# Silu of the recurrence's inputs and its gate as one ScalarE function, in pairs, and padded images that share their zero columns

## The chip, the cores and the metric

The kernel runs on one core of a Trainium2 chip. The metric is device microseconds (us) from launch to end; the median of three runs of the kernel before is 14450.43 us (14435.74 to 14463.01). The engines of the core work side by side, each through its own queue in order: TensorE (PE, matmuls, with its weight loads PEld), VectorE (DVE), ScalarE (ACT, table functions), GpSimd (POOL), and SyncE (SP), which here only issues transfers (DMA).

## The reference

32 images of 128 channels and 56 x 56 pixels, in float32, pass through four layers, each with a residual:

```python
# L0: group norm, then a 1x1 convolution whose weights are mixed per image by a small attention,
#     then three depthwise 3x3 convolutions with dilations 1, 3, 5
y = einsum('boi,bihw->bohw', agg_w, x) + agg_b
for dil in (1, 3, 5):
    out = out + silu(conv_general_dilated(y, ds_weight, padding=dil, rhs_dilation=dil) + ds_bias)
# L1: group norm, then a cubic B-spline of every element
# L2: group norm, linear attention over 8 heads, then a depthwise 3x3 convolution (dilation 1)
# L3: layer norm, then a selective state space recurrence along the 3136 pixels
xin, z = split(einsum('blc,ec->ble', xn, in_proj_w), 2)
xc = silu(conv_b + sum(xp[:, k:k + L] * conv_w[:, k] for k in range(4)))
dt, B, C = split(x_proj_w @ xc);  delta = softplus(dt_proj_w @ dt + dt_proj_b)
h = exp(delta * A) * h + delta * B * xc;  y = C . h + D * xc        # 256 channels x 16 states
out = out_proj_w @ (y * silu(z))
```

The change is about the two silu of L3, `silu(conv ...)` and `silu(z)`, and about the images with zero borders that L0 and L2 store for their depthwise convolutions.

## The kernel before

An image is held as 128 partitions (channels) by 3136 pixels and cut into seven chunks of 448 pixels (8 rows). Of each chunk the recurrence takes 16 steps; a step handles two groups of 128 rows (32 channels by 4 states each). Over 32 images this makes 224 chunks and 3584 steps. In one step:

- ScalarE computes the decays `da` with two Exp of 448 columns (`decay`); three buffers `da` take turns, so the decays of a step wait for the scan of three steps before;
- TensorE spreads the B row over the partitions into the PSUM tile `pb` (`b_rows`), and for every other step the C row, which ScalarE copies to `cb`;
- VectorE multiplies `rep` (a copy of delta*x that a transfer spread) with `pb` into `db`, which lies in one PSUM buffer, and runs `tensor_tensor_scan` over 904 columns into `h` (`state`);
- GpSimd multiplies `h` with `cb` into `hc` (`products`), and TensorE sums `hc` into `y` (`add`).

Around these steps lies all other work, of this chunk and of other images. `ssm_inputs` ("next") prepares the following chunk: 16 matmuls per half with the input projection (`winT`), silu into `xc`, the projection to `dbl`, softplus into `delta` and `du`, two transfers to DRAM, from which `rep` is fetched, and the layer norm of the chunk after that. `gate` ("gate") makes `sz = silu(z)`. "rest" is the spline and attention of the next image, and "conv" the L0 layer of the image after that.

A planner (`Plan`) sets the order. Every call is recorded as a `Work` with a price and a due time; `LEAD` shifts the due times by kind of work; `attempt` then takes, for each engine, the work that can begin first, where a work that needs another ScalarE table than the one loaded counts 0.6 us later. The order that comes out is written into each engine's queue and is fixed. The program's main loop (line 1505) covers six images a turn, five times, and the last two images follow.

`silu` computes with the tanh of half the argument: the weights `winT` and `wzT` are halved once at the start, ScalarE takes Tanh of the PSUM tile into `t`, and VectorE computes `(t + 1) * ps`. Because VectorE reads the PSUM tile too, the bias of the convolution has to be in it: a matmul of `cbT` (in the type float32r, with a high and a low part of the bias in rows 0 and 32) by a column of ones, broadcast over 448 columns, adds it. Tanh lies in the same table as Exp; Ln, used in softplus and in the layer norm, lies in another.

`padded` are two DRAM images with a border of five zeros on every side: rows of 66 floats. `store_rows` writes eight rows (seven in L2) through a buffer `yc`, and `load_stack` reads three shifted copies of eight rows for one depthwise convolution, 528 floats per channel each.

Of the kernel before, what the change touches and what calls it, by code (L numbers as in the profile page):

```python
# [13 lines left out]
F32 = mybir.dt.float32  # L14
# [5 lines left out]
P = 128  # L20
# [5 lines left out]
HALO = 5  # L26
PW = W + 2 * HALO
# [50 lines left out]
GATES = 5, 10  # L78
# [3 lines left out]
    "conv gpsimd att att": -21,  # L82
    "conv gpsimd attb att": -1,
    "conv gpsimd attr att": -9.5,
    "conv gpsimd pooled mv": -42,
    "conv gpsimd rs ve": -71,
    "conv gpsimd xt xt": 7,
    "conv scalar aggT mm": -21,
    "conv scalar att att": -52,
    "conv scalar part dwT": 11,  # L90
    "conv scalar vv mv": -6.5,
    "conv scalar yc mm": -1.5,
    "conv sync padded yc": -14,
    "conv sync stack padded": -3.5,
    "conv sync xt x_dram": 42,
    "conv tensor mm aggT": 9.5,
    "conv tensor mm fc1T": 22.5,
    "conv tensor mm gmat": 12,
    "conv tensor mm hid": -24,
    "conv tensor mm ident": -22,  # L100
    "conv vector aggb aggb": 35,
    "conv vector aggb attb": -11,
    "conv vector att mm": 13.5,
    "conv vector g t": -14.5,
    "conv vector hid mm": -33,
    "conv vector mg mm": 59,
    "conv vector mv st": -12.5,
    "conv vector mx att": -175.5,
    "conv vector mx mx": 36.5,
    "conv vector st xt": 1.5,  # L110
    "conv vector ve mm": -39.5,
    "gate scalar t mm": 0.5,
    "gate tensor mm wzT": 11,
    "gate vector sz t": -442,
    "next gpsimd delta delta": -7,
    "next gpsimd du delta": -51.5,
    "next gpsimd rstd cen": -38,
    "next gpsimd xn rstd": -62,
    "next gpsimd xn xn": -5.5,
    "next scalar cen mm": 2.5,  # L120
    "next scalar dbl mm": -253.5,
    "next scalar du du": -126,
    "next scalar du mm": -7.5,
    "next scalar rstd mm": -18.5,
    "next scalar rstd rstd": -47,
    "next scalar sq mm": -95,
    "next scalar t mm": -0.5,
    "next sync flat delta": -109,
    "next sync flat du": 7,
    "next tensor mm cbT": 2,  # L130
    "next tensor mm ctr": -3,
    "next tensor mm winT": -3.5,
    "next tensor mm xprojT": -1.5,
    "next vector xc t": 5.5,
    "rest gpsimd ab ve": -19.5,
    "rest gpsimd ind xt": -10.5,
    "rest gpsimd mcell mcell": -92,
    "rest gpsimd rs ve": 24,
    "rest gpsimd rstd cen": -12,
    "rest gpsimd xn": 3.5,  # L140
    "rest gpsimd xn rstd": 14.5,
    "rest gpsimd xt xt": 9,
    "rest scalar cen mm": -44,
    "rest scalar hats hats": 0.5,
    "rest scalar rstd mm": 11,
    "rest scalar rstd rstd": -56.5,
    "rest scalar sq mm": 9.5,
    "rest scalar top ab": -0.5,
    "rest scalar ws mm": -54.5,
    "rest scalar ws ws": -6.5,  # L150
    "rest scalar yc mm": -76.5,
    "rest sync flatx xt": -24.5,
    "rest sync padded yc": -1,
    "rest sync stack flatx": 7,
    "rest sync stack padded": -29.5,
    "rest tensor mm ctr": -10.5,
    "rest tensor mm gmat": 1,
    "rest tensor mm ident": -58,
    "rest tensor mm jmat": -41.5,
    "rest tensor mm wpT": 19.5,  # L160
    "rest tensor mm wqT": 11,
    "rest tensor mm ws": 21.5,
    "rest tensor mm wspl": -19,
    "rest tensor mm wv": 1.5,
    "rest vector ab mg": -42.5,
    "rest vector ab rs": 27.5,
    "rest vector bia bia": -16.5,
    "rest vector bia kneg": -73,
    "rest vector cb mm": 18,
    "rest vector cube sq": 2,  # L170
    "rest vector kb mm": -17,
    "rest vector mcell mg": 3.5,
    "rest vector mg mm": -141.5,
    "rest vector mv st": -11,
    "rest vector nm": 2.5,
    "rest vector nm mg": -2,
    "rest vector rden mm": -1,
    "rest vector rden rden": 1,
    "rest vector scl mm": 109.5,
    "rest vector st xt": 10.5,  # L180
    "rest vector ve mm": -12,
    "rest vector ws": -14,
    "rest vector ws mm": -61.5,
    "rest vector xt mm": 230,
    "scan gpsimd hc h": 7.5,
    "scan gpsimd last h": -20,
    "scan gpsimd rep": 108,
    "scan gpsimd rep last": 38,
    "scan scalar da rep": 2,
    "scan sync out_dram xt": -17.5,  # L190
    "scan sync rep flat": 20,
    "scan tensor mm outT": 1,
    "scan tensor y ddiag": -32,
    "scan tensor y ids": 0.5,
    "scan vector db rep": -65.5,
    "scan vector h da": -13.5,
    "scan vector sz sz": -2,
    "scan vector xt xt": 30,
    "sync rep flat": -23,
# [22 lines left out]
class Plan:  # L222
# [8 lines left out]
    TABLE = 1.28  # L231
# [62 lines left out]
    def price(self, w, engine, method, args, kw):  # L294
# [232 lines left out]

@with_exitstack
def tile_conv_stack(ctx: ExitStack, tc: tile.TileContext, out: bass.AP, x: bass.AP, w: dict):
# [166 lines left out]
    cbT = const.tile([P, DI * P], F32R, name="cbT")  # L696
    cbw = setup(DI * P, name="g")
    nc.vector.memset(cbw[:], 0.0)
    for r in (0, 32):
        nc.sync.dma_start(cbw[r : r + 1, :], w["convb"])  # L700
    nc.vector.tensor_scalar_mul(cbw[:], cbw[:], 0.5)
    nc.vector.tensor_copy(cbT[:], cbw[:])
    nc.vector.tensor_sub(cbT[32:33, :], cbw[32:33, :], cbT[32:33, :])
    onesr = const.tile([P, 1], F32R, name="onesr")
    nc.vector.tensor_scalar_add(onesr[:], one[:], 0.0)
# [30 lines left out]

    padded = [dramp.tile([P, PW * PW], F32, name=f"padded{k}") for k in range(2)]
    onesd = dramp.tile([1, NG * ROWS * PW], F32, name="onesd")
    flatx = [dramp.tile([P, L], F32, name=f"flatx{k}") for k in range(2)]
    flats = [dramp.tile([DI, 2 * P * CH], F32, name=f"flat{k}") for k in range(2)]  # L740
    zero = setup(HALO * PW, name="t")
    nc.vector.memset(zero[:], 0.0)
    for pd in padded:
        nc.sync.dma_start(pd[:, 0 : HALO * PW], zero[:])
        nc.sync.dma_start(pd[:, (HALO + H) * PW :], zero[:])
    ones = setup(NG * ROWS * PW // 48, name="g")
    nc.vector.memset(ones[:], 1.0)
    nc.sync.dma_start(onesd[:].rearrange("a (p f) -> (a p) f", p=48), ones[:48, :])
    ycs = [const.tile([P, ROWS, PW], F32, name=f"yc{k}") for k in range(2)]
    for yc in ycs:  # L750
        nc.vector.memset(yc[:], 0.0)

    plan.pitch = {pd[:].tensor.name: PW * PW for pd in padded} | {onesd[:].tensor.name: NG * ROWS * PW}
# [55 lines left out]
    turn = [0]  # L809

    def store_rows(pd, r0, rows, write):

        yc = ycs[turn[0] % 2]
        turn[0] += 1
        write(yc[:, 0:rows, HALO : HALO + W])
        o = (HALO + r0) * PW
        nc.sync.dma_start(pd[:, o : o + rows * PW], yc[:, 0:rows, :].rearrange("p r c -> p (r c)"))

    def load_stack(pd, j, dil, bias):

        t = stk.tile([P, NG, ROWS * PW], F32, tag="stack", name="stack")
        with plan.together():
            for k in range(3):
                o = (HALO + j * ROWS + (k - 1) * dil) * PW
                nc.sync.dma_start(
                    t[G * k : G * k + G], pd[:, o : o + ROWS * PW].rearrange("(c p) f -> p c f", c=NG)
                )
            if bias:
                nc.sync.dma_start(t[BIAS : BIAS + 1], onesd[:].rearrange("a (c f) -> a c f", c=NG))
        return t  # L830

    def depthwise(t, dil, weights, bias):

        ps = psum()
        for i in range(3):
            rows = BIAS + 1 if bias and i == 0 else BIAS
            o = HALO + (i - 1) * dil
            with plan.together(NG):
                for c in range(NG):
# [3 lines left out]
                        t[:rows, c, :].rearrange("p (r c) -> p r c", c=PW)[:, :, o : o + W],  # L843
# [7 lines left out]
    def dynamic_conv(xt, st):  # L851
# [64 lines left out]
        for i, (j, dil) in enumerate(steps):  # L916
# [5 lines left out]
            ps = depthwise(stacks[i], dil, dsT, True)  # L922
# [11 lines left out]
    def spline(xt, st, fx):  # L934
# [30 lines left out]
        def load_u(j):  # L965

            t = stk.tile([P, NG, ROWS * PW], F32, tag="stack", name="stack")
# [60 lines left out]
    def linear_attention(xt, st):  # L1028
# [94 lines left out]
        def conv(j):  # L1123
# [3 lines left out]
            ps = depthwise(stacks[j], 1, wpT, False)  # L1127
# [469 lines left out]
```

## Time and profile before

| | |
|---|---|
| median of three runs | 14450.43 us |
| the profiled execution's own time | 14452.59 us |
| its span, first to last instruction | 14450.8 us |
| VectorE busy | 13215.0 us (91%) |
| TensorE busy | 12803.1 us (89%) |
| GpSimd busy | 11322.3 us (78%) |
| ScalarE busy | 10980.4 us (76%) |
| DMA queue, share of 16 engines | 68.9% |
| ScalarE table loads | 512, 1283 ns each |
| mean granted TensorE clock | 0.953 |

Busy times are unions over an engine's instructions: neighbouring instructions overlap by about a tenth of a microsecond, so the sum of the durations is larger. A group of instructions is named by what it writes and reads (`xc<-v,mm` writes `xc` from `v` and `mm`), and because one line of the planner issues everything, nearly all groups carry the line L498. "idle before" is the time for which the engine stood still just ahead of the group, with what ended it.

### The profile page before, as it was taken

What the parts mean: (1) busy time and instruction counts of PE and PEld (TensorE: products, weight loads), DVE (VectorE), ACT (ScalarE), POOL (GpSimd) and SP (SyncE); (2) the same over time, 40 slices, a digit from 0 to 9 for tenths busy, and PEclk for the clock granted to TensorE, in tenths of its full rate; (3) what the DMA queues carried; (4) which work ended last, traced back from release to release, by engine and by line L of the source; (5) the groups of instructions that cost most, each with busy time, mean ns of one, the idle gap of its engine ahead of it and who ended that gap; (6) DMA issues with size and microseconds to landing.
All of it is one profiled execution on the core that took longest, in us unless ns stands there. A gap on an engine that the chain in (4) does not pass through costs nothing. (4 is left out here: it accounts for less than half of the span.)

```text
span 14450.8 us, 297216 instructions
## 1 busy us (share of the span) xinstructions
PE 12803.1 (89%) x115296; PEld 4186.4 (29%) x115296; DVE 13215.0 (91%) x12423; ACT 10980.4 (76%) x17959; POOL 11322.3 (78%) x10150
## 2 busy tenths in 40 slices
PE   7889999888999888998899988889998899988886
PEld 2222232323233222333222222222332233322221
DVE  2799999989999998999999989999998999999899
ACT  4787778877778876788877778777787777887675
POOL 2777788877788877888877878778887778887777
PEclk8999999999999999999999999999999999999998
DMA  7677677766777766776776777777766767777553
GB/s 166 147 164 161 157 168 163 158 155 158 162 169 160 162 159 153 165 163 157 166 159 157 163 159 159 161 159 166 168 156 154 160 157 169 162 161 163 132 115 74
DMA packets 1298106, 2263.05 MB, mean 157 GB/s; under 512 B 114549, under 2 KB 922872, under 8 KB 1295994
## 3 DMA queue, kind: packets, MB, share of 16 engines
q1 hardware_dynamic: 1296666, 2243.75, 68.9%
q8 instruction: 916, 15.01, 0.5%
q14 instruction: 524, 4.29, 0.1%
HBM read 1813.23 MB, written 430.08 MB: 155 GB/s over the span
## 5 line engine op out<-in xcount | busy, mean ns | idle before, releaser
L498 POOL TENSOR_TENSOR hc<-h,cb 128x896 f32<-128x896 f32 x3584 | 7544.2, 2108 | 625.0 <-PE y L498 301.8
L498 DVE TENSOR_TENSOR_SCAN h<-da,db 128x904 f32<-128x904 f32 x3584 | 7281.6, 2032 | 216.4 <-ACT da L498 13.2
L498 ACT ACTIVATE da<-rep,alog 128x448 f32<-128x448 f32 x7168 | 4409.8, 662 | 2093.9 <-DVE h L498 1729.1
L498 DVE TENSOR_TENSOR db<-rep,pb 128x904 f32<-128x904 f32 x3584 | 3937.9, 1099 | 392.5 <-PE pb L498 197.9
L498 PE MATMUL y<-hc,ids 128*32 128x448 f32 x14336 | 2251.1, 564 | 388.6 <-POOL hc L498 383.3
L498 PE MATMUL pb<-dbl,sel 128*32 128x452 f32 x14336 | 1919.9, 579 | 441.1 <-DVE db L498 385.3
L498 POOL COPY last<-h 128x2 f32<-128x2 f32 x3072 | 572.3, 188 | 2066.9 <-DVE h L498 1944.1
L498 PE MATMUL mm<-stack,dsT 96*32 96x448 f32 (+1 forms) x16128 | 1916.5, 563 | 83.2 <-ACT v L498 31.5
L498 POOL TENSOR_TENSOR xt<-xt,v 128x448 f32<-128x448 f32 x1344 | 1538.1, 1148 | 231.4 <-DVE v L498 190.2
L498 ACT ACTIVATE wide<-stack,bia 128x448 f32<-128x448 f32 x2688 | 1652.9, 661 | 0.8 <-DVE bia L498 0.8
L498 PE MATMUL mm<-xn,winT 128*32 128x448 f32 x14336 | 1608.6, 563 | 37.0 <-DVE v L498 16.7
L498 ACT ACTIVATE v<-mm 128x448 f32<-128x448 f32 x2016 | 1069.0, 533 | 545.6 <-PE mm L498 531.4
L498 PE MATMUL mm<-wide,wspl 128*32 128x448 f32 x12544 | 1327.0, 547 | 117.3 <-ACT wide L498 50.4
L498 ACT ACTIVATE wide<-wide,one,scl 128x1344 f32<-128x1344 f32 x896 | 1346.9, 1503 | 0.1
L498 PEld LDWEIGHTS y<-hc,ids 128*32 128x32 f32 x14336 | 564.2, 112 | 1648.6 <-POOL hc L498 872.6
L498 PE MATMUL mm<-dbl,sel 128*32 128x448 f32 x7168 | 922.7, 570 | 79.7 <-DVE sz L498 45.5
L498 PEld LDWEIGHTS mm<-stack,dsT 96*32 96x32 f32 (+1 forms) x16128 | 554.1, 112 | 1116.5 <-issue 946.5
L498 PEld LDWEIGHTS pb<-dbl,sel 128*32 128x32 f32 x14336 | 415.5, 112 | 1487.8 <-DVE db L498 1045.4
L498 PEld LDWEIGHTS mm<-xn,winT 128*32 128x32 f32 x14336 | 481.0, 113 | 898.9 <-issue 771.4
L498 PEld LDWEIGHTS mm<-wide,wspl 128*32 128x32 f32 x12544 | 410.3, 111 | 969.9 <-issue 658.2
L498 ACT COPY cb<-mm 128x448 f32<-128x448 f32 x896 | 470.5, 525 | 254.9 <-PE mm L498 187.8
L498 ACT ACT_TABLE_LOAD x512 | 656.9, 1283 | 8.8
(188 smaller groups left out, 13787.4 us busy)
## 6 DMA issues: line engine op xcount, KB each, us to landing
rep<-flat SPq DMA_DIRECT2D x1792, 448.0 KB
stack<-padded SPq DMA_DIRECT2D x2688, 264.0 KB
stack<-flatx SPq DMA_DIRECT2D x896, 224.0 KB
flat<-delta SPq DMA_DIRECT2D x224, 448.0 KB
flat<-du SPq DMA_DIRECT2D x224, 448.0 KB
padded<-yc SPq DMA_DIRECT2D x224, 264.0 KB
padded<-yc SPq DMA_DIRECT2D x256, 231.0 KB
xt<-x_dram SPq DMA_DIRECT2D x224, 224.0 KB
```

The source lines that it names most:

```text
L498: call.func(*map(self.bind, call.args), **{k: self.bind(v) for k, v in call.keywords.items()})
```

## The change

`gate` and the first part of `ssm_inputs` first make both PSUM tiles of a chunk and then, as one work of the planner, two `Silu` activations, directly into `sz` or `xc`. VectorE has no part in them. The bias of the convolution is a per-partition column `convb` of the activation; `cbT`, its matmuls and the halved weights are gone. The planner knows a third table, "silu". `GATES` has one place, so both halves of the gate come at step 5 of the chunk. L0's silu still goes through Tanh and VectorE.

`Padded` gives each of the two images its own halo (5 for L0, 1 for L2), its own two row buffers, and a pitch of `W + halo`: 61 or 57 floats. The zeros at the end of one row serve as those at the start of the next. `load_stack` reads 493 or 457 floats per channel instead of 528, and `depthwise` takes its rows at that pitch. The numbers in `LEAD` are other ones throughout.

```diff
-HALO = 5
-PW = W + 2 * HALO
+HALOS = (5, ROWS), (1, ROWS - 1)
+SPAN = ROWS * (W + 5) + 2 * 5
...
-GATES = 5, 10
+GATES = (5,)
...
-            if method == "activation" and args[2] in (AF.Exp, AF.Tanh, AF.Ln):
-                w.table = "ln" if args[2] == AF.Ln else "exp"
+            if method == "activation" and args[2] in self.TABLES:
+                w.table = self.TABLES[args[2]]
...
+class Padded:
+    def __init__(self, dram, sbuf, name, halo, rows):
+        self.halo, self.pitch, self.turn = halo, W + halo, 0
+        self.length = (H + 2 * halo) * self.pitch + halo
+        self.image = dram.tile([P, self.length], F32, name=name)
+        self.rows = [sbuf.tile([P, rows, self.pitch], F32, name=f"yc{halo}_{k}") for k in range(2)]
...
-        nc.vector.scalar_tensor_tensor(winT[:, k, :], winT[:, k, :], 0.5, wxT[:], ALU.mult, ALU.mult)
-    nc.vector.tensor_scalar_mul(wzT[:], wzT[:], 0.5)
...
+        nc.vector.tensor_mul(winT[:, k, :], winT[:, k, :], wxT[:])
+    convb = load("convb", [P, DI])
...
     def load_stack(pd, j, dil, bias):
-        t = stk.tile([P, NG, ROWS * PW], F32, tag="stack", name="stack")
+        t = stk.tile([P, NG, SPAN], F32, tag="stack", name="stack")
+        n = ROWS * pd.pitch + pd.halo
         with plan.together():
             for k in range(3):
-                o = (HALO + j * ROWS + (k - 1) * dil) * PW
+                o = (pd.halo + j * ROWS + (k - 1) * dil) * pd.pitch
                 nc.sync.dma_start(
-                    t[G * k : G * k + G], pd[:, o : o + ROWS * PW].rearrange("(c p) f -> p c f", c=NG)
+                    t[G * k : G * k + G, :, :n], pd.image[:, o : o + n].rearrange("(c p) f -> p c f", c=NG)
                 )
...
     def gate(xn):
+        pss = [psum() for _ in range(DI)]
         for db in range(DI):
-            ps = psum()
-            tiled(ps, wzT[:, db * P : (db + 1) * P], xn[:, DCONV - 1 :], True, True)
-            silu(sz[:, db, :], ps)
-            yield 0.8
+            tiled(pss[db], wzT[:, db * P : (db + 1) * P], xn[:, DCONV - 1 :], True, True)
+        with plan.together():
+            for db in range(DI):
+                nc.scalar.activation(sz[:, db, :], pss[db], AF.Silu)
+        yield 1.6
...
     def ssm_inputs(xt, k, norm):
...
+        pss = [psum() for _ in range(DI)]
         for db in range(DI):
             ch = slice(db * P, (db + 1) * P)
-            ps = psum()
             for i in range(DCONV):
-                tiled(ps, winT[:, i, ch], xn[:, i : i + CH], (i == 0), False)
-            nc.tensor.matmul(ps, cbT[:, ch], onesr[:].to_broadcast([P, CH]), start=False, stop=True)
-            silu(xc[:, db, :], ps)
-            yield 3.3
+                tiled(pss[db], winT[:, i, ch], xn[:, i : i + CH], (i == 0), (i == DCONV - 1))
+            if db < DI - 1:
+                yield 3.3
+        with plan.together():
+            for db in range(DI):
+                nc.scalar.activation(xc[:, db, :], pss[db], AF.Silu, bias=convb[:, db : db + 1])
+        yield 3.3
...
-                gates = Pieces("gate", gate(xns[k % 3]), 1.6, 2)
+                gates = Pieces("gate", gate(xns[k % 3]), 1.6, 1)
```

More of the change, by code (lines that the diff above doesn't have):

```diff
@@ L77 @@
 FIRST, SECOND = -2, -1
-GATES = 5, 10
+GATES = (5,)
 READY = 12
 LEAD = {
[L82 to L153, printed above, removed]
-    "rest sync stack flatx": 7,
[L155 to L161, printed above, removed]
@@ new lines @@
+    "conv gpsimd att att": -58,
+    "conv gpsimd attb att": -15.5,
+    "conv gpsimd attr att": -1,
+    "conv gpsimd pooled mv": -83.5,
+    "conv gpsimd pooled pooled": 16,
+    "conv gpsimd rs ve": 44.5,
+    "conv scalar aggT mm": 3,
+    "conv scalar att att": -18.5,
+    "conv scalar part dwT": -5.5,
+    "conv scalar t mm": -26,
+    "conv scalar vv mv": -2,
+    "conv scalar yc mm": -23,
+    "conv sync padded yc": 16,
+    "conv sync stack padded": 0.5,
+    "conv sync xt x_dram": 9,
@@ new lines @@
+    "conv tensor mm aggT": -6.5,
+    "conv tensor mm dsT": 3,
+    "conv tensor mm fc1T": 11,
+    "conv tensor mm gmat": 21,
+    "conv tensor mm ident": 8,
+    "conv vector aggb aggb": 30,
+    "conv vector aggb attb": 1,
+    "conv vector att mm": -0.5,
+    "conv vector g t": 12.5,
+    "conv vector hid mm": 35.5,
+    "conv vector mg mm": -96,
+    "conv vector mv st": -18.5,
+    "conv vector mx att": -23.5,
+    "conv vector mx mx": -25,
+    "conv vector st xt": -1.5,
+    "conv vector ve mm": -19,
@@ new lines @@
+    "gate scalar sz mm": -9,
+    "gate tensor mm wzT": 17,
+    "next gpsimd du delta": -186.5,
+    "next gpsimd rstd cen": -12,
+    "next gpsimd xn rstd": -12.5,
+    "next gpsimd xn xn": 43.5,
+    "next scalar cen mm": -59.5,
+    "next scalar dbl mm": -272.5,
+    "next scalar delta mm": -157,
+    "next scalar du du": -61,
+    "next scalar rstd mm": -26.5,
+    "next scalar rstd rstd": 20,
+    "next scalar sq mm": -7.5,
+    "next scalar xc mm": 28.5,
+    "next sync flat du": -11.5,
@@ new lines @@
+    "next tensor mm ctr": 2,
+    "next tensor mm dtT": -3.5,
+    "next tensor mm jmat": -114.5,
+    "next tensor mm winT": -10.5,
+    "next tensor mm xprojT": -1,
+    "rest gpsimd ab ve": -20.5,
+    "rest gpsimd ind xt": -14,
+    "rest gpsimd mcell mcell": -69,
+    "rest gpsimd rs ve": 57.5,
+    "rest gpsimd rstd cen": -46,
+    "rest gpsimd xn": 112.5,
+    "rest gpsimd xn rstd": 1,
+    "rest scalar cen mm": -104.5,
+    "rest scalar ctr cen": 1.5,
+    "rest scalar hats hats": 1.5,
@@ new lines @@
+    "rest scalar hats stack": -8,
+    "rest scalar rstd mm": 43.5,
+    "rest scalar rstd rstd": -2,
+    "rest scalar sq mm": 14.5,
+    "rest scalar top ab": 30.5,
+    "rest scalar vv mv": -5.5,
+    "rest scalar ws mm": -11.5,
+    "rest scalar ws ws": 27,
+    "rest scalar yc mm": -14.5,
+    "rest sync flatx xt": -14.5,
+    "rest sync padded yc": 30,
+    "rest sync stack flatx": 7,
+    "rest sync stack padded": -10.5,
+    "rest tensor mm ctr": -26.5,
+    "rest tensor mm gmat": -163,
@@ L162 @@
+    "rest tensor mm ident": 9,
+    "rest tensor mm jmat": 15,
+    "rest tensor mm wpT": 4.5,
+    "rest tensor mm wqT": 3,
     "rest tensor mm ws": 21.5,
     "rest tensor mm wspl": -19,
[L164 to L199, printed above, removed]
+    "rest tensor mm wv": -2,
+    "rest vector ab mg": 53.5,
+    "rest vector ab rs": 38.5,
+    "rest vector bia bia": 43.5,
+    "rest vector bia kneg": 8,
+    "rest vector cb mm": -25,
+    "rest vector cube sq": 13.5,
@@ new lines @@
+    "rest vector kb mm": -24.5,
+    "rest vector mcell mg": -1,
+    "rest vector mg mm": 5.5,
+    "rest vector mv st": 25,
+    "rest vector nm": 7.5,
+    "rest vector nm mg": -74,
+    "rest vector rden mm": 32.5,
+    "rest vector rden rden": -84.5,
+    "rest vector scl mm": 11.5,
+    "rest vector st xt": 6,
+    "rest vector ve mm": 7,
+    "rest vector ws mm": 16.5,
+    "rest vector xt mm": 32.5,
+    "rest vector xt xt": -94,
+    "scan gpsimd hc h": -6,
+    "scan gpsimd last h": -48.5,
@@ L200 @@
+    "scan gpsimd rep": 20,
+    "scan gpsimd rep last": 63,
+    "scan scalar cb mm": -23,
+    "scan scalar da rep": 12.5,
+    "scan sync out_dram xt": -4,
+    "scan sync rep flat": -16,
+    "scan tensor mm outT": 2,
+    "scan tensor mm sel": 1.5,
+    "scan tensor y ddiag": -2,
+    "scan tensor y ids": 3,
+    "scan vector db rep": -90.5,
+    "scan vector h da": 5,
+    "scan vector sz sz": 57,
+    "scan vector xt xt": 10,
+    "sync rep flat": -27.5,
 }
@@ L230 @@
     RATE, LANDING, LANES = 1.8e5, 1.8, 8
-    TABLE = 1.28
+    TABLE, TABLES = 1.28, {AF.Exp: "exp", AF.Tanh: "exp", AF.Ln: "ln", AF.Silu: "silu"}
     NEVER = 1e18
@@ L692, in tile_conv_stack @@
     for k in range(DCONV):
-        nc.vector.scalar_tensor_tensor(winT[:, k, :], winT[:, k, :], 0.5, wxT[:], ALU.mult, ALU.mult)
-    nc.vector.tensor_scalar_mul(wzT[:], wzT[:], 0.5)
[L696 to L705, printed above, removed]
+        nc.vector.tensor_mul(winT[:, k, :], winT[:, k, :], wxT[:])
+    convb = load("convb", [P, DI])
     nc.scalar.activation(amat[:], amat[:], AF.Exp)
@@ L733, in tile_conv_stack @@
     du = const.tile([P, DI, CH], F32, name="du")
-    padded = [dramp.tile([P, PW * PW], F32, name=f"padded{k}") for k in range(2)]
-    onesd = dramp.tile([1, NG * ROWS * PW], F32, name="onesd")
+    padded = [Padded(dramp, const, f"padded{h}", h, n) for h, n in HALOS]
+    onesd = dramp.tile([1, NG * SPAN], F32, name="onesd")
     flatx = [dramp.tile([P, L], F32, name=f"flatx{k}") for k in range(2)]
     flats = [dramp.tile([DI, 2 * P * CH], F32, name=f"flat{k}") for k in range(2)]
-    zero = setup(HALO * PW, name="t")
+    zero = setup(SPAN, name="t")
     nc.vector.memset(zero[:], 0.0)
     for pd in padded:
-        nc.sync.dma_start(pd[:, 0 : HALO * PW], zero[:])
-        nc.sync.dma_start(pd[:, (HALO + H) * PW :], zero[:])
-    ones = setup(NG * ROWS * PW // 48, name="g")
+        nc.sync.dma_start(pd.image[:, : pd.halo * pd.pitch], zero[:, : pd.halo * pd.pitch])
+        nc.sync.dma_start(pd.image[:, (pd.halo + H) * pd.pitch :], zero[:, : pd.halo * (pd.pitch + 1)])
+    ones = setup(NG * SPAN // 24, name="g")
     nc.vector.memset(ones[:], 1.0)
-    nc.sync.dma_start(onesd[:].rearrange("a (p f) -> (a p) f", p=48), ones[:48, :])
-    ycs = [const.tile([P, ROWS, PW], F32, name=f"yc{k}") for k in range(2)]
-    for yc in ycs:
+    nc.sync.dma_start(onesd[:].rearrange("a (p f) -> (a p) f", p=24), ones[:24, :])
+    for yc in padded[0].rows + padded[1].rows:
         nc.vector.memset(yc[:], 0.0)
-    plan.pitch = {pd[:].tensor.name: PW * PW for pd in padded} | {onesd[:].tensor.name: NG * ROWS * PW}
+    plan.pitch = {pd.image[:].tensor.name: pd.length for pd in padded} | {onesd[:].tensor.name: NG * SPAN}
     plan.pitch |= {fx[:].tensor.name: L for fx in flatx}
@@ L807, in silu @@
         nc.vector.scalar_tensor_tensor(dst, t[:], 1.0, ps, ALU.add, ALU.mult)
-    turn = [0]
     def store_rows(pd, r0, rows, write):
[L813 to L817, printed above, removed]
+        yc = pd.rows[pd.turn % 2]
+        pd.turn += 1
+        write(yc[:, 0:rows, pd.halo :])
+        o = (pd.halo + r0) * pd.pitch
+        nc.sync.dma_start(pd.image[:, o : o + rows * pd.pitch], yc[:, 0:rows, :].rearrange("p r c -> p (r c)"))
     def load_stack(pd, j, dil, bias):
-        t = stk.tile([P, NG, ROWS * PW], F32, tag="stack", name="stack")
+        t = stk.tile([P, NG, SPAN], F32, tag="stack", name="stack")
+        n = ROWS * pd.pitch + pd.halo
         with plan.together():
             for k in range(3):
-                o = (HALO + j * ROWS + (k - 1) * dil) * PW
+                o = (pd.halo + j * ROWS + (k - 1) * dil) * pd.pitch
                 nc.sync.dma_start(
-                    t[G * k : G * k + G], pd[:, o : o + ROWS * PW].rearrange("(c p) f -> p c f", c=NG)
+                    t[G * k : G * k + G, :, :n], pd.image[:, o : o + n].rearrange("(c p) f -> p c f", c=NG)
                 )
@@ L830, in load_stack, with depthwise @@
         return t
-    def depthwise(t, dil, weights, bias):
+    def depthwise(pd, t, dil, weights, bias):
         ps = psum()
@@ L836, in depthwise @@
             rows = BIAS + 1 if bias and i == 0 else BIAS
-            o = HALO + (i - 1) * dil
+            o = pd.halo + (i - 1) * dil
             with plan.together(NG):
@@ L842, in depthwise @@
                         weights[:rows, c, i, :],
-                        t[:rows, c, :].rearrange("p (r c) -> p r c", c=PW)[:, :, o : o + W],
+                        t[:rows, c, o : o + ROWS * pd.pitch].rearrange("p (r c) -> p r c", r=ROWS)[:, :, :W],
                         start=(i == 0),
@@ L921, in dynamic_conv @@
                 stacks.append(load_stack(pd, *steps[i + 1], True))
-            ps = depthwise(stacks[i], dil, dsT, True)
+            ps = depthwise(pd, stacks[i], dil, dsT, True)
             cols = slice(j * CH, (j + 1) * CH)
@@ L965, in load_u @@
         def load_u(j):
-            t = stk.tile([P, NG, ROWS * PW], F32, tag="stack", name="stack")
+            t = stk.tile([P, NG, SPAN], F32, tag="stack", name="stack")
             cols = slice(j * CH, (j + 1) * CH)
@@ L1126, in conv @@
             cols = slice(j * CH, (j + 1) * CH)
-            ps = depthwise(stacks[j], 1, wpT, False)
+            ps = depthwise(img, stacks[j], 1, wpT, False)
             nc.vector.scalar_tensor_tensor(xt[:, cols], ps, wpb[:, 0:1], xt[:, cols], ALU.add, ALU.add)
@@ L1565, in _layout @@
         "convwT": c(a["L3_conv_conv_w"].T).reshape(1, DCONV * DI * P),
-        "convb": a["L3_conv_conv_b"].reshape(1, DI * P),
+        "convb": halves(a["L3_conv_conv_b"]),
         "xprojT": halves(xproj_columns(a["L3_conv_x_proj_w"].T)),
```

## The prediction

> **What bounds the kernel now.** I read the engines' busy times first, then the table of stages, then who waits for whom on VectorE, and last the timeline of single steps. The main loop is even: in a stretch of 3000 us from its middle VectorE works 2811 us, and TensorE, which comes next, 2696.
>
> ```profile
> PE 12803.1 (89%) x115296; PEld 4186.4 (29%) x115296; DVE 13215.0 (91%) x12423; ACT 10980.4 (76%) x17959; POOL 11322.3 (78%) x10150
> 6000.00:9000.00 3000.00, 2696.27 (x24566) 885.34 (x24562) 2810.63 (x2622) 2348.59 (x3844) 2410.61 (x2158) 0.96 0.71 161
> ```
>
> The groups say what fills VectorE, and that ScalarE runs ahead: most of its idle time ahead of `da` ends with a scan, so the decays wait for a free buffer and not the scan for decays. The waits of VectorE confirm it, with 13.2 us in the whole span for decays.
>
> ```profile
> L498 DVE TENSOR_TENSOR_SCAN h<-da,db 128x904 f32<-128x904 f32 x3584 | 7281.6, 2032 | 216.4 <-ACT da L498 13.2 <-POOL hc L498 6.0 <-POOL xn L498 2.9
> L498 DVE SCALAR_TENSOR_TENSOR xc<-v,mm 128x448 f32<-128x448 f32 x448 | 270.6, 604 | 75.1 <-ACT v L498 74.6
> L498 DVE SCALAR_TENSOR_TENSOR sz<-v,mm 128x448 f32<-128x448 f32 x448 | 269.9, 604 | 40.8 <-ACT v L498 40.1 <-PE mm L498 0.7
> L498 ACT ACTIVATE da<-rep,alog 128x448 f32<-128x448 f32 x7168 | 4409.8, 662 | 2093.9 <-DVE h L498 1729.1 <-PEq L1505 79.2 <-DVE rden L498 63.5
> L498 PE MATMUL mm<-onesr,cbT 128*128 128x448 f32 x448 | 204.2, 456 | 0.0
> L498 ACT ACT_TABLE_LOAD x512 | 656.9, 1283 | 8.8
> DVE db L498 <- PE pb L498: 197.9, 174, 2.9
> ```
>
> The timeline gives the price of a step: start and duration of each VectorE instruction.
>
> ```profile
> 3147.25 2.04 DVE L498 TENSOR_TENSOR_SCAN h<-da,db 128x904 f32<-128x904 f32 x1
> 3149.39 1.10 DVE L498 TENSOR_TENSOR db<-rep,pb 128x904 f32<-128x904 f32 x1
> 3150.62 2.04 DVE L498 TENSOR_TENSOR_SCAN h<-da,db 128x904 f32<-128x904 f32 x1
> 3152.58 0.60 DVE L498 SCALAR_TENSOR_TENSOR sz<-v,mm 128x448 f32<-128x448 f32 x1
> 3153.09 1.10 DVE L498 TENSOR_TENSOR db<-rep,pb 128x904 f32<-128x904 f32 x1
> 3154.29 2.04 DVE L498 TENSOR_TENSOR_SCAN h<-da,db 128x904 f32<-128x904 f32 x1
> ```
>
> A bare step takes 3.37 us from scan to scan (3.34 in the median of 302 such steps between 3000 and 9000 us), although its two instructions last 3.14: each waits a moment for the one before. A step with one instruction of 0.6 us between takes 3.67 (3.66 in the median). So an added instruction costs 0.32 to 0.34, since it fills that gap; a second in the same place costs 0.5. The mean step of the loop is 3.94 us, of which some 0.17 are waits for other engines. 3584 steps of 3.94 are 14,120 us; with the 417 us ahead of the first scan and a shorter end this is the span.
>
> **The change part by part**, against the profiled execution's 14452.59 us (2 us above the median of 14450.43).
>
> VectorE loses 448 `xc` and 448 `sz` instructions. Four fifths of those I could place stand alone in their gap (0.33 us), the rest beside another one (0.55): 0.37 on average, 896 x 0.37 = 330 us. Bounds: 896 x 0.32 = 287 and, by their full duration, 896 x 0.604 = 541; the step periods decide. With them go the waits ahead of them, 75 + 41 = 116 us. The longest, 17.7 us, lies ahead of the first scan, where `xc` is awaited in any case, and others only move to the next user; I take 80 of 0 to 116. Together -410 us.
>
> ScalarE: 896 Tanh become 896 Silu. No row has a Silu. The nearest is Tanh from PSUM, 533 ns; with a bias column the row `du<-mm,dtb` has 628. So +95 ns on 448 of them, 43 us. What matters is the tables. In the instruction order of the changed kernel ScalarE has 1255 loads where the order of before has 515 (512 recorded): the `sz` pair mostly follows the Ln pair, so it adds one load, the `xc` pair two. 740 x 1.283 = 949 us, and ScalarE comes to 10980 + 949 + 43 = 11,972 us, 84% of an unchanged span.
>
> ```profile
> 6041.89 0.58 ACT L498 ACTIVATE yc<-mm,rden 128x392 f32<-128x392 f32 x1
> 6042.48 1.28 ACT L498 ACT_TABLE_LOAD   x1
> 6043.77 1.04 ACT L498 ACTIVATE du<-du,one 128x896 f32<-128x896 f32 x1
> 6044.83 1.28 ACT L498 ACT_TABLE_LOAD   x1
> ```
>
> From the end of `yc` at 6042.47 to the start of `du` at 6043.77 a load costs 1.30 us in all. The Trainium skill, "ScalarE: Activation LUTs", section "What ACT_TABLE_LOAD costs", speaks harder against the change: 1283 ns for the load and about 1380 ns for a drain, 2.66 us for each switch. By that, 740 loads would be an estimated 1968 us and ScalarE would be as full as VectorE; the rows show the first part and no drain.
>
> How much of this reaches the scan is a matter of where the loads lie. The planner counts a change of table as 0.6 us and so, once `silu` or `ln` is loaded, prefers every ready work that needs no table to the decays. In the changed order the eleventh step of each image shows it: between the decays of the tenth step and its own stand two loads (2.6), the `sz` and `xc` pairs and three other reads of PSUM (3.3), twelve spline biases at 0.57 (6.8), four wide Relu at 1.41 (5.6), small ones and its own decays (1.7): 20.0 us. The cover: the tenth step's decays cannot begin before the scan three steps earlier has ended, and take 1.2; the eleventh scan would be due four steps less one scan after that same end, 4 x 3.85 - 2.04 = 13.4. It comes 21.2 - 13.4 = 7.8 us late, every image. In before's order the same place has no such block, except in the first image of a turn of the loop (19 us, at most 6.9 of wait in the trace). Four more stretches, of 13 to 14 us with a pair between two loads, are short by 2.4, 1.7, 2.5 and 0.8 us if steps take 3.6, and by nearly nothing if they take 3.85. Over 30 images (the last have no spline beside them): 240 + 40 = 280 us. Bounds: nothing, if VectorE stands there anyway for the attention's small reductions, and (7.8 + 7.4) x 32 = 490, or some 620 if each ScalarE instruction is held up by 5% by its inputs. I take +280, near the middle, because the block of 20 us is certain and the smaller ones are not.
>
> What waits behind: in ScalarE's queue the PSUM reads of the other layers, so PSUM tiles come free later, and a pair holds two of the four `mm` tiles where one was held, while TensorE makes the second half (16 matmuls, about 2.5 us). `pb` for the next steps is queued behind those matmuls. This can cost 0 to 100 us; I leave it in the bound.
>
> TensorE loses 448 matmuls of 456 ns, 204 us of 12,803. VectorE waits 197.9 us for `pb` in all, so the gain lies between 0 and 198; these matmuls are 1.6% of TensorE's work, and most of those waits come from order: 20 us.
>
> Padding: 2016 loads shrink from 264 to 246.5 KB and 672 to 228.5, which is 61 of 2244 MB, 2.7% of a queue that is 69% busy. `stack<-padded` ends 20 us of TensorE's waits and 23 end with `stack<-onesd`, none of them VectorE's beyond 6; two more row buffers remove 9 us of ScalarE's waits for `yc`. Between 0 and 40 us; other engines' work covers it, 0. The gate at step 5 alone: `sz` is free from step 2 on, when the output projection of the last chunk has read it, and needed from step 10 on; 0, and a few us a chunk if it were late.
>
> Sum: -410 + 280 - 20 = -150 us, 14452.6 - 150 = 14,303, said as 14,300.
>
> **The rivals.** *ScalarE becomes the bound* (slower): one mechanism, the decays late behind blocks of loads and spline work. It decides once the waits of `h` for `da` pass 430 us, 13.4 an image. With the 490 us of all five stretches at fast steps and VectorE's relief at its lower end (287 + 40 + 20 = 347) the time is 14,595; at 620, 14,725. For it: ScalarE at 84% with blocks of 20 us, and only three buffers `da`. Against: 1729 us in which ScalarE waits for scans today.
>
> *The tables are hidden*: the decays run far enough ahead, and the full relief is left, 14452.6 - 430 = 14,022. For it: 13.2 us of waits for decays today. Against: the 20 us block, and TensorE, which would be at 12,599 of 14,022 or 90%, more than its 88.6% now.
>
> *A wash*: what VectorE saves, ScalarE's blocks return, or the saved time falls into gaps that another wait then fills; 14,450.
>
> **How the numbers follow.** The forecast (14,080 to 14,420, its own range) has 0.43, the full relief (below 14,080) 0.15, the wash 0.10 and the late decays 0.32. This gives faster by over 0.2% (29 us, about what a measurement of this kernel can tell from no change: its three runs span 27) 0.58, within it 0.10, slower 0.32. The range leaves out a part of the fullest relief and the far end of the late decays: 13,980 to 14,620.
>
> **What would show it.** Right: about 1250 table loads at 1.28 us; VectorE busy near 12,670 us and its bare steps still 3.34; ScalarE near 11,970; waits of `h` for `da` of 200 to 400 us, most of them 7 to 8 us long and one per image at its eleventh step; no `cbT`. Wrong: loads that cost 2.6 us from neighbour to neighbour; waits for `da` past 430 us or spread over every chunk; or the waits of `db` for `pb` grown past 300 us, which would put the loss on PSUM tiles held by the pairs.

## The result, and the profile after

The changed kernel takes 14,517.78 us (median of six, 14,510.97 to 14,524.25) where the kernel before takes 14,451.15 in the same comparison: a ratio of 1.0046, 95% interval 1.0033 to 1.0059. It is slower by 67 us; the forecast was a gain of 150. The time lies inside the stated range, on the other side of no change, where the rival of the late decays was put.

The busy times and the stretch 6000 to 9000 us, from the page and the table of stages of the changed kernel:

```profile
PE 12618.4 (87%) x114848; PEld 4126.4 (28%) x114848; DVE 12846.1 (89%) x11523; ACT 11967.2 (82%) x18699; POOL 11335.8 (78%) x10150
6000.00:9000.00 3000.00, 2643.07 (x24326) 864.43 (x24322) 2717.80 (x2416) 2535.88 (x3970) 2400.05 (x2145) 0.96 0.68 155
```

VectorE lost 900 instructions and 369 us of busy time, ScalarE gained 987 us. In equal time VectorE, still the fullest engine, now works 2718 us where it worked 2811: it waits more. The groups and VectorE's waits say for what:

```profile
L500 DVE TENSOR_TENSOR_SCAN h<-da,db 128x904 f32<-128x904 f32 x3584 | 7286.7, 2033 | 494.6 <-ACT da L500 169.2 <-POOL hc L500 35.2 <-ACT sz L500 32.6
L500 ACT ACTIVATE da<-rep,alog 128x448 f32<-128x448 f32 x7168 | 4411.5, 665 | 1547.9 <-DVE h L500 1275.6 <-PEq L1509 79.8 <-DVE ve L500 77.0
L500 ACT ACT_TABLE_LOAD x1252 | 1606.3, 1283 | 21.7
L500 ACT ACTIVATE xc<-mm,convb 128x448 f32<-128x448 f32 x448 | 260.1, 631 | 16.0 <-PE mm L500 13.6
L500 ACT ACTIVATE sz<-mm 128x448 f32<-128x448 f32 x448 | 221.0, 542 | 21.4 <-PE mm L500 19.0
DVE h L500 <- ACT da L500: 169.2, 101, 11.7
DVE hid L500 <- PE mm L500: 90.6, 32, 3.4
DVE mx L500 <- ACT att L500: 66.6, 32, 2.8
DVE att L500 <- PE mm L500: 30.0, 31, 1.0
```

The scan waits 169 us for decays instead of 13, mostly in four places of an image, about 31 to 47 us in each. `hid`, `mx` and `att` are the small steps of L0's attention, and each waits 31 or 32 times, once per image. In 25 of the 30 images of the loop (not in the first of each turn of six) they meet in one place, the eleventh step of an image, where only 6 of the 169 us lie. ScalarE's timeline there, cut to what matters:

```profile
3550.73 1.28 ACT L500 ACT_TABLE_LOAD   x1
3552.03 0.98 ACT L500 ACTIVATE sz<-mm 128x448 f32<-128x448 f32 x2
...
3563.43 2.92 ACT L500 ACTIVATE wide<-wide,one,scl 128x1344 f32<-128x1344 f32 x2
3566.23 1.15 ACT L500 ACTIVATE xc<-mm,convb 128x448 f32<-128x448 f32 x2
3567.40 1.28 ACT L500 ACT_TABLE_LOAD   x1
3568.69 0.67 ACT L500 ACTIVATE da<-rep,alog 128x448 f32<-128x448 f32 x1
3569.27 0.28 ACT L500 ACTIVATE att<-att,mx 128x4 f32<-128x4 f32 x1
```

and VectorE's in the same moments, with two lines of GpSimd:

```profile
3558.20 2.02 DVE L500 TENSOR_TENSOR_SCAN h<-da,db 128x904 f32<-128x904 f32 x1
...
3563.06 1.87 POOL L500 TENSOR_SCALAR v<-xt,top,cpad 128x448 f32<-128x448 f32 x1
3564.90 0.19 POOL L500 TENSOR_TENSOR pooled<-pooled,rs 128x1 f32<-128x1 f32 x1
3565.77 0.21 DVE L500 TENSOR_SCALAR hid<-mm,fc1b 33x1 f32<-33x1 f32 x1 [3.42 <-PE mm L500]
3566.96 0.16 DVE L500 TENSOR_TENSOR att<-mm,fc2b 128x4 f32<-128x4 f32 x1 [0.99 <-PE mm L500]
...
3569.58 0.16 DVE L500 TENSOR_REDUCE mx<-att 128x1 f32<-128x4 f32 x1 [2.08 <-ACT att L500]
...
3570.14 2.04 DVE L500 TENSOR_TENSOR_SCAN h<-da,db 128x904 f32<-128x904 f32 x1 [0.20 <-ACT da L500]
```

From the first load to the end of the decays ScalarE is taken up for 19.4 us, and from scan to scan this step takes 11.94 us, in 6.69 of which VectorE stands still: 167 us in the 25 images. In the order of before the same step of these images takes 3.73 us, without a wait. Only 0.20 of the wait is booked on `da`, because VectorE has already spent the rest on the attention's steps that stand ahead of the scan in its queue. These are late by another path than the decays: `hid` needs GpSimd's `pooled`, which ends at 3565.09, and a matmul behind it, and `att` another matmul. The order of before has the same steps spread over several scans, with other work of VectorE between.

It helps to split the mean step between 3000 and 9000 us into work and waits: work is 3.34 us, plus 0.33 for a VectorE instruction of about 0.6 us in a gap, 0.52 for each further one in the same gap and 0.1 for a tiny one; the waits are what the timeline has beyond that. All rows come from the profiles of the kernels told of below.

| kernel | step, us | work | waits |
|---|---|---|---|
| before | 3.938 | 3.770 | 0.167 |
| changed | 3.961 | 3.684 | 0.278 |
| relief_only | 3.868 | 3.680 | 0.189 |
| tanh_same_order | 3.928 | 3.685 | 0.243 |
| relief_silu_xc | 4.036 | 3.679 | 0.357 |

The work fell by 0.086 us a step, 310 us over 3584 steps, as forecast. The waits rose by 0.111, which is 397. Together this is 87 us of loss where the whole kernels differ by 67, so a stretch scaled up is off by some 20. The experiments are about those waits.

### The profile page after: what moved, and what is told of

Read it like the earlier page. It is cut to its first block, busy times and chain, and to the rows that moved or that the text cites. A ratio compares the mean times of both kernels' runs of the same rounds, so it can differ in the third digit from the quotient of the medians.

```text
span 14510.8 us, 296450 instructions
## 1 busy us (share of the span) xinstructions
PE 12618.4 (87%) x114848; PEld 4126.4 (28%) x114848; DVE 12846.1 (89%) x11523; ACT 11967.2 (82%) x18699; POOL 11335.8 (78%) x10150
## 5 line engine op out<-in xcount | busy, mean ns | idle before, releaser
L500 DVE TENSOR_TENSOR_SCAN h<-da,db 128x904 f32<-128x904 f32 x3584 | 7286.7, 2033 | 494.6 <-ACT da L500 169.2
L500 PE MATMUL y<-hc,ids 128*32 128x448 f32 x14336 | 2156.1, 558 | 475.3 <-POOL hc L500 420.4
L500 PE MATMUL pb<-dbl,sel 128*32 128x452 f32 x14336 | 1847.1, 578 | 331.0 <-DVE db L500 297.3
L500 PE MATMUL mm<-stack,dsT 96*32 96x448 f32 (+1 forms) x16128 | 1826.1, 562 | 98.3 <-DVE v L500 61.3
L500 PEld LDWEIGHTS y<-hc,ids 128*32 128x32 f32 x14336 | 531.5, 112 | 1732.0 <-POOL hc L500 841.1
L500 PE MATMUL mm<-dbl,sel 128*32 128x448 f32 x7168 | 871.6, 556 | 52.0 <-DVE v L500 25.7
L500 ACT ACTIVATE v<-mm 128x448 f32<-128x448 f32 x1120 | 605.3, 540 | 239.3 <-PE mm L500 237.9
L500 PEld LDWEIGHTS mm<-xn,winT 128*32 128x32 f32 x14336 | 518.1, 112 | 946.5 <-issue 760.6
```

The costliest lines, as they stand in the source:

```text
L500: call.func(*map(self.bind, call.args), **{k: self.bind(v) for k, v in call.keywords.items()})
```

## The experiments

Theory: the loads, and the blocks in which the planner puts them, take back VectorE's relief. Rivals: the new order costs by itself, the padding costs, or the relief is smaller than it looks. "Same order" means that the planner is shown the old works, so that every other instruction stands where it stood. The edits are shown shortened; a comment stands for what is left out.

**relief_only: VectorE's relief by itself.**

```diff
# before.py, for sz and xc
         nc.scalar.activation(t[:], ps, AF.Tanh)      # xc: written into xc itself
-        nc.vector.scalar_tensor_tensor(dst, t[:], 1.0, ps, ALU.add, ALU.mult)
+        # planned, never issued; sz is then made from xc and y
```

> The kernel before in its own order, with the 896 VectorE instructions of the two silu never issued: Tanh writes xc itself, and sz is made from xc instead (neither is the reference's silu). No table load is added and nothing is moved, so this is the prediction's term of -410 us by itself. Prediction: 330 us from the steps and 80 of waits, 14,040. By the bare step periods alone 14,120. Rival: another engine's order takes over (TensorE, busy 89%), so that most of the saved time comes back as waits of db for pb: 14,300 or more.

Measured: 14,220.22 us (14,209.17 to 14,237.90), ratio 0.9841 (0.9828 to 0.9855): -234 us, between the theories. The work of a step fell just as forecast (0.091). But the waits did not fall with the instructions in front of which they stood, they rose by 0.022. From the waits of VectorE:

```profile
DVE db L498 <- PE pb L498: 269.0, 217, 5.3
DVE xt L498 <- PE mm L498: 116.0, 55, 17.8
DVE st L498 <- POOL xt L498: 55.3, 76, 1.3
```

They were 198, 80 and 38 before, so these three rose by 125. The 116 us ahead of `xc` and `sz` were not saved: as much came back ahead of other instructions, whose inputs had not become faster.

**relief_no_bias: the same without the bias matmuls.**

```diff
-            nc.tensor.matmul(ps, cbT[:, ch], onesr[:].to_broadcast([P, CH]), start=False, stop=True)
+            # planned, never issued
```

> As relief_only (order of before, the 896 VectorE instructions of the two silu not issued, sz and xc not the reference's), and the 448 bias matmuls by cbT are not issued either (the bias is left out). This is the prediction's TensorE term by itself: 20 us beyond relief_only's 14,220, so about 14,200. Rival 'TensorE is next': relief_only returned 176 of the predicted 410 us because TensorE's queue became the bound; then the 204 us of matmuls come off nearly whole and the time is 14,030 to 14,100.

Measured: 14,243.29 us (14,242.83 to 14,245.50), ratio 0.9858 (0.9843 to 0.9873), no better than relief_only. VectorE still waits for results of TensorE (285 us for `pb`, where relief_only has 269), but not because TensorE has too many matmuls: leaving out 204 us of them is worth nothing here, and the forecast's 20 were too many.

**pad_only_same_order: the padding by itself.**

```diff
# before.py with Padded; both halos 5, one pair of row buffers, prices held at those of before
+HALOS = (5, ROWS), (5, ROWS)
```

> The kernel before with rows of 61 floats that share their zeros, in both images (so the second image's loads have 493 floats and not 457), one pair of row buffers as before, and the planner's prices and regions held so that the order of all engines is that of before. Prediction: 0, between 0 and 40 us of gain, 14,410 to 14,455, and the DMA share falls from 69% to about 66%. Rival 'padding': the overlapping reads or the pitch cost something, and the 67 us of loss come from here: 14,500 or more.

Measured: 14,436.92 us (14,424.57 to 14,466.74), ratio 0.9989 (0.9980 to 0.9998). The DMA queue's share falls from 68.9 to 67.1%. The padding gives some 17 us, at the edge of what can be told from nothing, and it costs nothing. Of the kernels here that compute the whole reference it is the fastest, and the only one below both the kernel before and the changed one.

**tanh_same_order and tanh_xc_same_order: the loads by themselves.** The changed kernel in its own order, with fewer loads.

```diff
-                nc.scalar.activation(sz[:, db, :], pss[db], AF.Silu)
+                nc.scalar.activation(sz[:, db, :], pss[db], AF.Tanh)     # not in tanh_xc_same_order
-                nc.scalar.activation(xc[:, db, :], pss[db], AF.Silu, bias=convb[:, db : db + 1])
+                nc.scalar.activation(xc[:, db, :], pss[db], AF.Tanh, bias=convb[:, db : db + 1])
# the planner still gives sz and xc a table of their own
```

> The changed kernel with Tanh in place of its Silu, while the planner still prices a table of its own: every instruction stands where it stood, and only the 740 added table loads are gone (sz and xc hold tanh, so the output is not the reference's). Theory 'loads': the loss is the time of the loads inside ScalarE's blocks. The block ahead of the eleventh step's decays shrinks from 20.0 to 17.4 us and ScalarE's busy time falls by about 950 us, waits of VectorE on ScalarE's results (da, att, sz) fall by half, and the time falls by 200 to 330 us, to 14,190 to 14,320. Rival 'order': the new order costs by itself, whatever the loads take; the block still is 4 us too long; the time stays above 14,430.

> The changed kernel in its own order with Tanh for xc and Silu for the gate alone (xc is not the reference's): 857 loads, against 1255 with both and 515 with neither. If every load costs alike, 342 of 740 give 60 of the 129 us: 14,449. If the loads of xc cost more, since xc stands at the head of the chain to the next chunk's du and its pair is shut in by two loads, 14,400 to 14,430; if those of the gate, which stand right behind Ln at the late decays, 14,470 to 14,500.

Measured: 14,389.08 us without any of them (14,388.77 to 14,398.71, ratio 0.9959, 0.9945 to 0.9972), 14,425.16 with the gate's alone (14,418.27 to 14,437.69, ratio 0.9981, 0.9972 to 0.9990). So in this order the 740 loads cost 129 us, the gate's 342 of them 36 and those of `xc` 93. The busy time of ScalarE is 944 us less, and yet only 129 of them were on the path. Both theories fell short: the loads cost less than 200, and without them the kernel is still 169 us slower than relief_only. The waits of VectorE show what the order alone does:

```profile
DVE h L500 <- ACT da L500: 169.9, 104, 11.7
DVE hid L500 <- PE mm L500: 90.4, 31, 3.4
```

Waits for decays and for `hid` are what they are in the changed kernel (169.2 and 90.6), though the loads are gone. The eleventh step of the image shown above, now on VectorE:

```profile
3523.51 2.03 DVE L500 TENSOR_TENSOR_SCAN h<-da,db 128x904 f32<-128x904 f32 x1
...
3531.07 0.21 DVE L500 TENSOR_SCALAR hid<-mm,fc1b 33x1 f32<-33x1 f32 x1 [3.42 <-PE mm L500]
3532.27 0.16 DVE L500 TENSOR_TENSOR att<-mm,fc2b 128x4 f32<-128x4 f32 x1 [0.99 <-PE mm L500]
...
3533.18 0.16 DVE L500 TENSOR_REDUCE mx<-att 128x1 f32<-128x4 f32 x1 [0.36 <-ACT att L500]
3533.37 0.16 DVE L500 RECIPROCAL mx<-mx 128x1 f32<-128x1 f32 x1
3533.74 2.04 DVE L500 TENSOR_TENSOR_SCAN h<-da,db 128x904 f32<-128x904 f32 x1 [0.20 <-ACT da L500]
```

It takes 10.23 us for 11.94, so without the loads 1.7 us of the step are gone, 43 us in 25 images and a third of the 129. With the gate's loads alone, in tanh_xc_same_order, it is back at 11.94. The other 5.0 us of waits stay. Two paths end there within 0.2 us of each other: the attention's chain by GpSimd and TensorE (its last step ends at 3533.53) and ScalarE's spline work, behind which the decays end at 3533.70. Either alone would hold the scan, and no run takes them apart.

**due_first: the blocks broken up.**

```diff
-                    late = at + 0.6 * (w.table is not None and w.table != table)
+                    late = at + 0.0 * (w.table is not None and w.table != table)
-    "scan scalar da rep": 12.5,
+    "scan scalar da rep": -29,
# and "next scalar du du" -16, "rest scalar hats hats" 12, "rest scalar sq mm" -11, "scan scalar cb mm" -38
```

> The changed kernel with the planner's 0.6 us against a change of table set to 0, so that among works that can begin now the due time decides, and with five numbers of LEAD set anew, decays earlier (-29 for 12.5) among them. All the work is the same, with a few more table loads (about 1350). Theory 'loads in blocks': what costs is that table-free work is pushed ahead of due decays while silu is loaded; with the blocks broken up the decays are late by 2 to 4 us an image and no longer by 12, and the time falls by 150 to 260 us, to 14,260 to 14,370. Rival 'loads anywhere': 740 loads cost what they cost wherever they stand: 14,480 to 14,600.

Measured: 15,328.89 us (15,323.85 to 15,349.94), ratio 1.0609 (1.0594 to 1.0623). A clear miss. The waits for decays did go, from 169 us to 3.5, but:

```profile
DVE v L500 <- ACT v L500: 518.7, 403, 16.4
DVE xt L500 <- PE mm L500: 405.2, 186, 16.1
DVE db L500 <- PE pb L500: 384.8, 254, 6.1
```

Work of the other layers came late instead, and VectorE, whose queue is in order, stands ahead of it just the same. Early decays did not help in this order. The run changes six numbers at once and has 131 loads more (1383), so it prices none of them.

**tanh_replanned, no_leads_before, no_leads_after: what an order is worth.**

```diff
# tanh_replanned: after.py with AF.Tanh for both, priced as Tanh
# no_leads_before, no_leads_after
+LEAD = {}
```

> The changed kernel with Tanh in place of its Silu and the planner told so: no table of its own, 740 loads fewer, the planner free to place everything anew under the same numbers in LEAD (sz and xc hold tanh). Theory 'loads': with neither loads nor blocks around them the time is at or below that of the same order without loads, 14,389, and may reach 14,220. Theory 'order': the numbers in LEAD fit one set of works only; any other set is ordered worse by some hundred us, whatever it saves: 14,500 to 14,800.

> The kernel before with an empty LEAD: due times as the planner works them out. Theory 'order': worse by 300 to 700 us than before's 14,451, which shows how much the numbers are worth. Rival: within 100 us of it.

> The changed kernel with an empty LEAD. If the change costs by its nature (loads, pairs, blocks), it is slower than the kernel before with an empty LEAD, by 0.5 to 2%. If the loss comes from numbers in LEAD that suit the changed kernel less well than the old ones suited the old kernel, it is faster than that, by 1% or more (the relief of 234 us).

Measured: tanh_replanned 14,787.31 us (14,775.70 to 14,795.42, ratio 1.0232, 1.0218 to 1.0246); no_leads_before 14,991.19 (14,989.44 to 15,003.85, ratio 1.0378, 1.0362 to 1.0394); no_leads_after 15,327.70 (15,317.04 to 15,329.82, ratio 1.0606, 1.0589 to 1.0622). The same work as tanh_same_order, planned anew under the same numbers, is 398 us slower. The numbers in `LEAD` are worth 544 us to the kernel before and 810 to the changed one, and without them the change costs 336 us, 2.2%. So, as far as an empty `LEAD` can tell, the loss is not that the new numbers are worse than the old ones: they hide most of a larger loss.

**relief_silu_xc and silu_before_order: the loads in an order that was not made for them.**

```diff
# relief_only, and Silu in place of Tanh for xc; silu_before_order: for sz too, with the full weights
-        nc.scalar.activation(dst, ps, AF.Tanh)
+        nc.scalar.activation(dst, ps, AF.Silu)
```

> As relief_only (order of before, 896 VectorE instructions of the two silu not issued), with Silu in place of Tanh for xc alone, which puts 786 more table loads into that order (the changed kernel has 740 more than before); xc and sz are not the reference's. Theory 'cheap loads': a load costs what it costs in the changed order, 129 us for 740, so 14,220 + 137 = 14,357, and the rest of the change's loss is its order alone. Theory 'the order pays for the loads': in an order not made for them the same loads cost more, 250 to 450 us, 14,470 to 14,670, and the changed order's 169 us are what it spends on making room for them.

> Both silu as ScalarE's Silu (full weights, bias still by the matmul of cbT), in the order of the kernel before: nothing paired, 2121 table loads, 1606 more than before; computes the whole reference. 'Cheap loads' at 0.174 us each: 14,220 + 280 = 14,500. 'The order pays': ScalarE at 13,060 us busy of 14,500 is at 90%, decays wait in every chunk; 14,800 to 15,300, and pairing is what makes the change bearable.

Measured: relief_silu_xc 14,769.91 us (14,760.21 to 14,780.70, ratio 1.0221, 1.0207 to 1.0235), silu_before_order 15,538.80 (15,520.57 to 15,548.09, ratio 1.0750, 1.0735 to 1.0764). Against relief_only that is 550 us for 786 loads and 1319 for 1606: 0.70 and 0.82 us each, more than either theory said, and four to five times the 0.174 of the changed order. The waits, in relief_silu_xc:

```profile
L498 ACT ACT_TABLE_LOAD x1298 | 1665.3, 1283 | 44.3 <-DVE h L498 22.6
DVE v L498 <- ACT v L498: 540.6, 325, 17.2
DVE db L498 <- PE pb L498: 319.6, 260, 4.6
DVE xt L498 <- PE mm L498: 226.9, 110, 17.8
```

In relief_only the same three were 257, 269 and 116 us. The scan waits 22 us for decays here. This fits loads of 1.28 us that push back ScalarE's other work, for which VectorE and then TensorE wait; the waits alone do not prove that chain.

## Why the prediction was wrong, point by point

**The sum by the runs.** -234 (relief alone) + 169 (to the changed order, without its loads; padding, pairs and the missing bias matmuls are in it) + 129 (the loads in it) = +64, and the change measured +67. Each term is the difference of two neighbours in one chain of kernels, so that they add up is no test of them.

**VectorE's steps** were right: 330 us forecast, 0.091 x 3584 = 324 in relief_only. The 80 us of waits that were to go with them were wrong in sign, and outside their bounds of 0 to 116: waits rose by 0.022 x 3584 = 79. A wait ahead of a removed instruction was counted as the price of that instruction, and it was the price of an input that the next user still waits for. This step is 159 of the 217 us by which the forecast missed. VectorE's busy time was put near 12,670 and came to 12,846 in the changed kernel (369 us less, where the durations of what was removed add up to 541), because neighbours overlap.

**The loads.** Their number (1255 for 1252 recorded), ScalarE's busy time (11,972 for 11,967; it is 83% of an unchanged span, not 84) and the length of the eleventh step's block (20.0 us for 19.4) came as worked out. A load costs 1.30 us from neighbour to neighbour again (3550.73 to 3552.03), not the 2.66 of the Trainium skill's "ScalarE: Activation LUTs", section "What ACT_TABLE_LOAD costs".

**The term of +280 for ScalarE** has a total that came near, 298 for order and loads together, but partly by luck. In the eleventh step it had the place right: VectorE waits 167 us there. It had 7.8 us in each of 30 images (234, summed as 240), and they are 6.7 in 25. It had them as one cause, the decays behind ScalarE's block. By VectorE's waits 110 of them are for `hid` and `att`, which come by TensorE; 52 are for ScalarE's `att` and 5 for decays; and the loads are worth 43. That VectorE might stand there for the attention's small steps was named, as a reason for a cost of nothing; in the new order it stands there, loads or not, and in the old one it does not. The loads in all are 129, and the other 169 are order, for which the prediction had no term of its own: outside the eleventh step it had 40 us. due_first and relief_silu_xc show that late decays are only one form of the loss: in other orders the scan hardly waits for them, and VectorE waits for `v`, `pb` and `xt`. Of the signs named, 200 to 400 us of waits of `h` for `da`, mostly at the eleventh step, did not come: they are 169, and 6 there.

**TensorE** was to give 20 us and gave nothing; **padding** was put at 0 and gave 17, within its bounds of 0 to 40.

So the miss has one main step, the relief: -410 forecast, -234 measured. With the measured -234, the forecast's own +280 and its -20 for TensorE the sum would have been 26 us of loss, on the right side but no more than could be told from no change. The rival of the late decays named the side; its price of 14,595 at the least was 77 us too high, and its deciding point, 430 us of waits of `h` for `da`, was drawn too narrowly: 169 us of them were enough, since other waits carried the rest.

**What stays open:** the 169 us were not split into pairs, the single gate place and the numbers in `LEAD`, because any such edit makes the planner order everything anew, and that moves the time by more (398 us in tanh_replanned). Whether another set of numbers would bring the changed kernel below the one before was not tried. relief_silu_xc supports that the order pays 169 us to make the loads cheap; it does not prove that it must.

## What to carry to other kernels

One kernel shows this, so take it as a thing to check: when an in-order engine is 90% busy and each of its neighbours 75 to 90%, price a removed instruction by the period of the steps with and without it, and count none of the waits ahead of it as gain unless their source gets faster too. Work that is moved to an engine with idle time is not free because that time is idle: a table load of 1.3 us cost 0.17 us in an order made for it and 0.70 and 0.82 in one that was not. In a kernel with a tuned order, test a cost with the order held, or the new order will be what is measured.

## What the runs showed of the hardware that was not expected

In most of these runs the granted TensorE clock is lower where TensorE is busy for less of the span: 0.962 at 89% (relief_only), 0.950 at 87% (changed), 0.926 at 84% (silu_before_order). It is no strict order: no_leads_before has 0.933 at 87%, no_leads_after 0.935 at 85%. silu_before_order has the same 115,296 matmuls as the kernel before, and TensorE is busy 13,129 us with them at 0.926 instead of 12,803 at 0.953. Leaving out 448 matmuls of 456 ns (relief_no_bias) went with a lower clock, 0.955 where relief_only has 0.962, and with only 58 us less of TensorE's busy time, where 204 were taken away. So matmuls that are removed need not come off in full; why the clock does this was not tried.

Silu costs what Tanh costs: 542 ns from PSUM, where Tanh takes 533 in the kernel before and 536 in the same place in tanh_same_order; with a bias column 631, where Tanh takes 626 there and 628 had been read from another function.
